# Softmax denominators of a batched attention kernel: the sum over partition quarters moved from a TensorE product to ScalarE copies and VectorE additions

## The chip, the cores and the metric

One Trainium2 core runs the whole kernel. The time is device microseconds (us) of one launch; the number that counts is the median over runs. The core has five instruction queues that run at the same time[...]: TensorE (PE, matrix products; its weight loads are shown apart as PEld), VectorE (DVE), ScalarE (ACT), GpSimd (POOL) and SyncE (SP), which issues the transfers. Each queue runs its instructions in the order in which they were written; an instruction that waits holds up all that stand behind it on its engine.

## What is computed

The input is 16 batches of 1024 nodes with 256 channels, in float32, and one 1024 x 1024 adjacency matrix. Cut to what matters:

```python
diff = c_adj[:, None, :] - c_adj[:, :, None]            # channel means of the nodes
A    = abs(abs(sigmoid(diff) - 0.5) - 0.5) * 2.0
g    = relu((fea @ (adj * A_s)) * para)                 # A_s: A made symmetric
k, v = x @ kv_w                                         # 4 heads of 64 channels
out  = softmax(q @ k.T * scale) @ v                     # q = g, by heads
x    = layernorm(x + out)
h    = relu(x @ w1_loop + adj @ (x @ w1_neigh) + b1)    # graph convolution 1
h    = relu(h @ w2_loop + adj @ (h @ w2_neigh) + b2)    # graph convolution 2
x    = layernorm(x + (x + h) * 0.5)
```

## The kernel before

The batches run one after another in a software pipeline. While batch b is in its attention, the queries, keys and values of batch b + 1 are prepared, and the graph convolutions of earlier batches are run in between: the first convolution of batch b - 1 (`c1`) and the second of batch b - 2 (`c2`) are one joint product, `Joined.run`. Batches 2 to 14, thirteen of them, have all of this and take the same path through `run()`; batches 0, 1 and 15 take others.

**Attention.** The scores of a head pair and one half of the nodes make a unit; there are four (`UNITS`). A unit's exponentials lie in eight tiles of 128 x 1024, where the partition is the key node and the columns are 512 query nodes of one head and 512 of the other. VectorE adds the eight tiles up (`collect`, L776 and L778), transposes the sum in blocks of 32 x 32 (`turned_sum`, L785) and sums over 32 columns (`part_sum`, L791). So `den_part` holds, for each unit, 32 columns on 128 partitions: the 128 partitions are four quarters of 32, each with a partial sum over a quarter of the key nodes. The denominators are the sums over the four quarters. `denominators` (L846) makes them with one TensorE product: `fold`, a 128 x 128 matrix of ones at places that agree modulo 32, times `den_part`, into a PSUM tile; then two reciprocals (L857) take the half of the columns that belongs to each head into `rden`. `add_output` (L859) multiplies the attention's output by `rden` and adds it to the activations.

**The order around the change.** In `both_units(1, ...)` the last unit's output (`av`, L803) is transposed (L835) as soon as TensorE has it, then `part_sum` of that unit follows, then the function `third`: two `scalar_tensor_tensor` instructions on VectorE, `q.times_adj(0)` and `q.times_adj(TJ)` (L613), for the next batch. GpSimd then works at `both.left` (L1323 to L1326) and `q.left` (L661 to L664), eight additions and subtractions of 128 x 512. `both.run` issues seven products of four matrix instructions each (eight records), into three PSUM tiles named `first`, `second` and `third`. What matters here is its beginning: ScalarE fills `third` with a stored sum (L1353); product 1 goes into `first`; ScalarE copies `first` to `p1` (L1355); product 2 is added onto `third`; product 6 is added onto `first`, and so it may not start before `p1` has been copied. At the point `turn_to(1)`, between product 1 and product 2, stand the likeness functions of the next batch on ScalarE (L607, L608), `att.denominators(0, 1)` and `att.add_output(0)`.

**Buffers.** All tiles of 128 x 1024 come from one pool of 31 buffers (`row_tile`). The schedule is written by hand, but which of the 31 buffers a tile gets is settled when the program is built. A tile waits for the last instructions that used its buffer's former tile. `p1` is half of such a row tile (`snap`), and the adjacency rows that `times_adj` reads are such tiles too. The pool `work` with the tag `o` has one buffer.

A float32 matrix product shows in the profile as two records.

Of the kernel before, what the change touches and what calls it, by code (L numbers as in the profile page):

```python
# [10 lines left out]
F32 = mybir.dt.float32  # L11
# [7 lines left out]
def kernel(  # L19
# [31 lines left out]
    nc = tc.nc  # L51

    B, N, C = x.shape
    P = 128
    NT = N // P
    NC = C // P
    HEADS = 4
    HD = C // HEADS
    HID = w1_loop.shape[1]
    FB = 512  # L60
    NJ = N // FB
    TJ = FB // P
# [7 lines left out]
    S = 32  # L70
    NB = N // S

    LIFT = 32.0
    UNITS = [(pair, j) for pair in range(NC) for j in range(NJ)]
    Q = P // S
# [3 lines left out]
    work = ctx.enter_context(tc.tile_pool(name="work", bufs=1))  # L79
# [88 lines left out]
    def sum_inner_weights():  # L168
        t = row_tile("w1_sums")
        a11, a12, a21, a22 = (w[:, cc, :] for w in (w1n_sb, w1l_sb) for cc in range(NC))  # L170
        s1, s2, s3, s4 = (t[:, ts(n, P)] for n in range(4))
        nc.gpsimd.tensor_add(s1, a21, a22)
        nc.gpsimd.tensor_sub(s2, s1, a11)
        nc.gpsimd.tensor_sub(s3, a11, a21)
        nc.gpsimd.tensor_sub(s4, a12, s2)
        nc.sync.dma_start(out=w1_sums, in_=t[:, 0:FB])
# [35 lines left out]
    def store(n, rows):  # L212
        for h in range(2):
            nc.sync.dma_start(out=far_adj[n][h], in_=rows[h])
# [10 lines left out]
    def adj_sums(quarters, k):  # L225
        for step in adj_sum_steps(quarters, k):
            step()

    def adj_sum_steps(quarters, k):

        w11, w12, w21, w22 = (of_rows(quarters[ij], k) for ij in QUARTERS)
        t13, t24 = (row_tile(f"adjT_{n}_{k}") for n in (13, 24))
        t = {1: t13[:, 0:FB], 3: t13[:, FB:N], 2: t24[:, 0:FB], 4: t24[:, FB:N]}

        def put(n, a, b):
            nc.vector.tensor_sub(t[n], a, b)
            nc.sync.dma_start(out=far_adj[n][k // 2][:, ts(k % 2, FB)], in_=t[n])

        return (lambda: (put(1, w12, w11), put(3, w22, w12)), lambda: put(2, w22, t[1]), lambda: put(4, w21, t[2]))
# [9 lines left out]
    def channel_major(blocked, name):  # L249

        dst = work.tile([P, NC, N], F32, tag="xT", name=name, bufs=2)
        for cc in range(NC):
            nc.vector.transpose(dst[:, cc, :], blocked[cc])
        return dst
# [90 lines left out]
    def by_node(t):  # L345
        return t.rearrange("p (bn r) -> p bn r", r=S)
# [382 lines left out]
    class Attention:  # L729
# [116 lines left out]
        def denominators(self, *pairs):  # L846
# [8 lines left out]
            for s in range(2):  # L855
                rows = slice(s * HD, (s + 1) * HD)
                nc.vector.reciprocal(rden[rows], den[rows, :, s, :])  # L857

        def add_output(self, pair):  # L859
            o = by_node(self.o.pop(NJ * pair))  # L860
            nc.vector.tensor_mul(o, o, self.rden[:, ts(pair, NB)].unsqueeze(2).to_broadcast([P, NB, S]))
            dst = by_node(self.xB[pair])
            nc.vector.tensor_add(dst, dst, o)
# [541 lines left out]
    def run():  # L1405
# [11 lines left out]
        q = Queries(0, x_first)  # L1417
# [47 lines left out]
        for b in range(B):  # L1465
            more = b + 1 < B
            att = Attention(b, xB, qT, kT, v)
            c1, c2, c3 = (convs.get(b - k) for k in (1, 2, 3))
            both = Joined(c1, c2) if c2 else None
# [4 lines left out]
            if more:  # L1474
                q = (FastQueries if c1 else Queries)(b + 1, xb)
# [6 lines left out]
            def weigh_first():  # L1482
                q.times_adj(0)
                q.times_adj(TJ)
                q.right(0)

            def two_units(pair, before_second=lambda: None):
                u = NJ * pair
                att.outputs(u, half_psum, turned=False)
                att.turn(u)  # L1490
                att.outputs(u + 1, turned=False)
                before_second()
                att.turn(u + 1)

            if more and not c1:
                att.both_scores(0)
                clip()
                NodeSums(q, xb, str(b + 1)).all()
                two_units(0)
                att.both_scores(1)  # L1500
                for t in range(3):
                    q.load(t)
                    q.weigh(t)
                two_units(1)
            elif more and not both:
                att.scores(0)
                att.outputs(0)
                NodeSums(q, xb, str(b + 1)).all()
                kv = KeysValues(b + 1, channel_major(blocked, f"xT_{b + 1}"))
                att.scores(1)  # L1510
                kv.sums()
                att.add(0)
                att.outputs(1)
                for t in (0, TJ):
                    q.load(t)
                c1.inner()
                q.left(nc.gpsimd)
                for t in (0, TJ):
                    q.likeness(t)
                for ij, n in QUARTERS.items():  # L1520
                    store(n, quarters[ij])
                c1.first(quarters, lambda: (att.add(1), adj_sums(quarters, 1), adj_sums(quarters, 2), weigh_first()))
                c1.turn_blocks()
                att.scores(2)
                att.outputs(2)
                for t in (1, TJ + 1):
                    q.load(t)
                    q.likeness(t)
                    q.times_adj(t)
                sum_inner_weights()  # L1530
                att.scores(3)
                for t in (2, TJ + 2, 3, TJ + 3):
                    q.load(t)
                for t in (2, TJ + 2, 3, TJ + 3):
                    q.likeness(t)
                q.right(1)
                att.add(2)
                att.outputs(3)
            elif more:
                nodes = None  # L1540

                def sums():
                    nonlocal nodes
                    nodes = NodeSums(q, xb, str(b + 1))
                    if c3:
                        c3.squares_aside()
                    c2.load_x()
                    c1.load_inner()

                def summed():  # L1550
                    c1.inner_sums()
                    if c3:
                        c3.deviation_aside()

                def turn_next():
                    nonlocal xT_next
                    xT_next = channel_major(blocked, f"xT_{b + 1}")

                xT_next = None

                def before_convolution():
                    both.fetch("00", "10")
                    for t in (0, TJ):
                        q.load(t)
                        q.likeness(t)
                    c1.load_t1()
                    both.fetch(2, 3)

                att.both_units(0, sums, lambda: nodes.turn(), summed=summed)
                nodes.line()  # L1570
                nodes.row()
                c1.fast_inner(turn_next)
                att.both_units(1, before_convolution, third=lambda: (q.times_adj(0), q.times_adj(TJ)))
                both.left(nc.gpsimd)
                q.left(nc.gpsimd, blocked)
                kv = KeysValues(b + 1, xT_next)
                both.fetch(1)
                for t in (1, TJ + 1):
                    q.load(t)
                both.fetch(4, "11")  # L1580

                def more_weights():
                    for t in (2, TJ + 2, 3, TJ + 3):
                        q.load(t)
                        q.likeness(t)
                    if c3:
                        c3.finish_aside(out[b - 3])

                both.run({1: (lambda: q.likeness(1), lambda: q.likeness(TJ + 1), lambda: att.denominators(0, 1),
                              lambda: att.add_output(0)),  # L1590
                          2: (lambda: att.sum_output(0), lambda: att.add_output(1)),
                          6: (lambda: q.right(0),),
                          4: (lambda: att.sum_output(1), lambda: q.times_adj(1), lambda: q.times_adj(TJ + 1)),
                          3: (more_weights, lambda: q.right(1))},
                         last=nc.gpsimd)
                c1.turn_blocks()
                if b + 2 < B:
                    c2.sums_aside()
            else:
                att.both_units(0, c1.load_inner, summed=c1.inner_sums)  # L1600
                c1.fast_inner()
                att.both_units(1, third=lambda: att.add_pairs(0))
# [57 lines left out]
            elif more:  # L1660
# [11 lines left out]
                first, second, third = adj_sum_steps(quarters, 3)  # L1672
# [17 lines left out]
        both = Joined(c1, c2)  # L1690
# [16 lines left out]
    with tc.manual_schedule():  # L1707
        run()
# [14 lines left out]
    with tc.If(count < P):  # L1723
        with tc.For_i(0, B, 1) as b:
            xb = load_x(b, "z")
            xT = channel_major(load_blocked(b, "z"), "xT_z")
            q = Queries("z", xb)
# [50 lines left out]
```

## Time and profile before

| | us |
|---|---|
| median of 3 runs (2111.35 to 2114.17) | 2112.22 |
| the profiled execution | 2112.32 |
| its span in the profile | 2110.5 |
| PE busy | 2096.5 (99%) |
| DVE busy | 1890.5 (90%) |
| ACT busy | 1247.0 (59%) |
| POOL busy | 364.4 (17%) |

The busy times are of the span. The span is 1.8 us shorter than the profiled execution. The granted TensorE clock is 0.999 of full speed. In the windows of the timeline every line is one instruction or a run of like ones: start, duration of the run from its first start to its last end, engine, source line, operation, out<-in, shapes and count; in brackets stands how long the engine was idle before it, and what ended that.

### The profile page before, as it was taken

Reading aid. Unit: us, or ns where it says so; the run is one execution under the profiler, and the core shown is the slowest. Engines: PE = TensorE matmul, PEld = TensorE weight load, DVE = VectorE, ACT = ScalarE, POOL = GpSimd, SP = SyncE. Lnnn points to the kernel's source line nnn. Section 1 sums busy time; section 2 is a strip of 40 time slices with the busy share of each in tenths; the row PEclk is TensorE's granted clock in tenths of the full one; section 3 lists DMA queues with packets and bytes.
Section 4 is the critical chain, followed back from the end, with each engine's and each line's share of the span. In section 5 each row is a group of like instructions: output and inputs, shape, how many; then the busy total and the mean of one; then the engine's idle time right before and its main releaser. Section 6 shows DMA issues by size and latency. Waiting matters only on the chain.

```text
span 2110.5 us, 24762 instructions
## 1 busy us (share of the span) xinstructions
PE 2096.5 (99%) x8360; PEld 996.7 (47%) x8360; DVE 1890.5 (90%) x2226; ACT 1247.0 (59%) x2112; POOL 364.4 (17%) x224
## 2 busy tenths in 40 slices
PE   9999999999999999999999999999999999999998
PEld 5354434445354453544535444354443534445355
DVE  6899998989989899898998989989899898989885
ACT  5844574556756566564765747557475584655523
POOL 2011103131021311213122031210312103131022
PEclk9999999999999999999999999999999999999999
DMA  9495756766648776477865768656586564966455
GB/s 220 114 184 185 146 142 199 139 215 146 173 167 160 241 132 195 155 143 241 142 204 153 142 221 174 204 132 155 195 175 216 144 155 173 183 216 131 145 186 175
DMA packets 688694, 364.99 MB, mean 173 GB/s; under 512 B 550704, under 2 KB 629936, under 8 KB 688560
## 3 DMA queue, kind: packets, MB, share of 16 engines
q1 hardware_dynamic: 688288, 363.07, 67.0%
q8 instruction: 68, 1.11, 0.2%
q14 instruction: 66, 0.54, 0.1%
q10 hardware_dynamic: 272, 0.26, 0.0%
HBM read 305.46 MB, written 57.80 MB: 172 GB/s over the span
## 4 chain that ended last, share of the span: by engine, by line
PE 97%; DVE 2%; DMA 0%; issue 0%; SPq 0%; ACT 0%; DVEq 0%; POOLq 0%
PE s L757 21%; PE av L803 20%; PE hu_ps L1332 17%; PE g_ps L702 16%; PE v_ps L463 5%; PE k_ps L459 5%; PE in_ps L997 4%; PE hu_ps L1134 4%; PE g_ps L621 3%; DVE acc L778 1%; PE h_ps L1045 1%; PE u_ps L1074 1%; PE h_ps L1134 1%; PE t_ps L971 0%; DMA x<-in_x_dram 0%
## 5 line engine op out<-in xcount | busy, mean ns | idle before, releaser
L778 DVE TENSOR_TENSOR acc<-acc,pr 128x1024 f32<-128x1024 f32 x384 | 481.4, 1254 | 34.0 <-DVE acc L776 0.9
L757 PE MATMUL s<-qT,kT 64*128 64x512 f32 x2048 | 448.7, 592 | 0.0
L803 PE MATMUL av<-pr,v 128*64 128x512 f32 x2048 | 447.0, 594 | 0.0
L764 ACT ACTIVATE pr<-s 128x1024 f32<-128x1024 f32 x392 | 390.9, 1117 | 58.1 <-PE s L757 58.1
L757 PEld LDWEIGHTS s<-qT,kT 64*128 64x128 f32 x2048 | 195.2, 187 | 241.0 <-issue 191.2
L803 PEld LDWEIGHTS av<-pr,v 128*64 128x64 f32 x2048 | 144.0, 137 | 297.3 <-issue 269.2
L1332 PE MATMUL hu_ps<-adj,R 128*128 128x512 f32 x480 | 213.6, 592 | 0.0
L376 POOL TENSOR_TENSOR rstd<-rstd,neg_half 128x32 f32<-128x32 f32 x16 | 88.3, 5522 | 564.5 <-DVE rstd L374 564.5
L613 DVE SCALAR_TENSOR_TENSOR wg<-wg,adj 128x1024 f32<-128x1024 f32 x128 | 169.0, 1359 | 3.6 <-ACT wg L608 3.6
L762 ACT ACTIVATE pr<-s 128x512 f32<-128x512 f32 x240 | 142.5, 703 | 0.0
L607 ACT ACTIVATE wg<-c_row,c_sums 128x1024 f32<-128x1024 f32 x120 | 139.7, 1164 | 2.6 <-DVE accB L785 1.0
L1332 PEld LDWEIGHTS hu_ps<-adj,R 128*128 128x128 f32 x480 | 90.0, 190 | 107.1 <-issue 99.2
L608 ACT ACTIVATE wg<-wg 128x1024 f32<-128x1024 f32 x128 | 135.5, 1058 | 4.1
L1332 PE MATMUL hu_ps<-adj,t 128*128 128x512 f32 x240 | 109.2, 598 | 0.0
L702 PE MATMUL g_ps<-wg,x 128*128 128x512 f32 x224 | 107.7, 593 | 0.0
L702 PE MATMUL g_ps<-T,xB 128*128 128x512 f32 x208 | 107.3, 597 | 0.0
L702 PE MATMUL g_ps<-wg,xB 128*128 128x512 f32 x208 | 106.2, 592 | 0.0
L1355 ACT COPY snap<-hu_ps 128x512 f32<-128x512 f32 x15 | 8.8, 586 | 157.4 <-PE hu_ps L1332 136.1
L1195 POOL TENSOR_TENSOR rstd<-rstd,neg_half 128x8 f32<-128x8 f32 x12 | 19.6, 1637 | 457.2 <-DVE rstd L1194 457.2
L1323 POOL TENSOR_TENSOR R<-h 128x512 f32<-128x512 f32 x14 | 20.7, 1480 | 433.5 <-PE av L803 407.3
L776 DVE TENSOR_TENSOR acc<-pr,pr 128x1024 f32<-128x1024 f32 x64 | 78.0, 1219 | 14.1 <-ACT pr L764 12.9
L785 DVE STREAM_TRANSPOSE accB<-acc 128x1024 f32<-128x1024 f32 x64 | 79.7, 1245 | 3.1
(301 smaller groups left out, 3298.9 us busy)
## 6 DMA issues: line engine op xcount, KB each, us to landing
adj<-adjT SPq DMA_DIRECT2D x210, 512.0 KB
adj<-in_adj_dram SPq DMA_DIRECT2D x128, 512.0 KB
para<-in_L_gnn_para_dram SPq DMA_DIRECT2D x32, 512.0 KB
xB_a<-in_x_dram SPq DMA_DIRECT2D x128, 128.0 KB
x1d<-xB_a SPq DMA_DIRECT2D x128, 128.0 KB
x<-x1d SPq DMA_DIRECT2D x16, 1024.0 KB
xB<-in_x_dram SPq DMA_DIRECT2D x120, 128.0 KB
x<-in_x_dram SPq DMA_DIRECT2D x15, 1024.0 KB
```

The costliest lines, as they stand in the source:

```text
L459: nc.tensor.matmul(dst, self.a[0][n], self.w[n], start=not again, stop=True, skip_group_check=again)
L463: nc.tensor.matmul(dst[:, ts(t, P)], self.w[n][:, ts(t, P)], self.a[1][n], start=not again and t == 0, stop=True, skip_group_check=again o ...
L607: nc.scalar.activation(wg, self.c_row, AF.Abs, bias=self.c_col[:, t:t + 1], scale=-1.0)
L608: nc.scalar.activation(wg, wg, AF.Tanh, scale=-0.5 / C)
L613: nc.vector.scalar_tensor_tensor(wg, wg, 1.0, self.adj.pop(t), op0=ALU.add, op1=ALU.mult)
L702: nc.tensor.matmul(self.p[n], x_n[:, k, :], w_n, start=(k == 0), stop=(k == TJ - 1))
L757: nc.tensor.matmul(halves[s], self.kT[rows, pair, ts(mt, P)], self.qT[rows, pair, ts(j, FB)], start=True, stop=True)
L762: nc.scalar.activation(pr[:, ts(s, FB)], halves[s], AF.Exp)
L764: nc.scalar.activation(pr, ps, AF.Exp)
L778: nc.vector.tensor_add(self.acc, self.acc, prs[mt])
L803: nc.tensor.matmul(pav[s * HD:(s + 1) * HD, :], self.v[:, mt, pair * P + s * HD:pair * P + (s + 1) * HD], prs[mt][:, ts(s, FB)], start=(mt ...
L1332: nc.tensor.matmul(dst, self.x[n][:, k, :], of_rows(rows, k), start=(start and k == 0), stop=(k == TJ - 1), skip_group_check=again)
```

## The change

Three functions take the place of `denominators(0, 1)` in batches 2 to 14. The other batches keep the product.

- `den_shift`, first thing in `third`: two ScalarE copies of 64 x 64 bring the columns of each head from the other 64 partitions.
- `den_halves`, between the two `times_adj`: two VectorE additions of 64 x 64 add them to the partitions' own columns. After it, partition halves are summed, and each head's columns lie on the head's own 64 partitions.
- `den_quarters`, first thing at `turn_to(1)`: four ScalarE copies of 32 x 64 exchange neighbouring quarters, one VectorE addition of 128 x 64 sums them, one reciprocal of 128 x 64 fills `rden`.

```diff
+        def den_shift(self):
+            t = work.tile([P, FB], F32, tag="o", name=f"den_{self.b}")
+            self.den = [t[:, ts(k, NC * NB)] for k in range(3)]
+            part = self.part.rearrange("p u (s h) -> p u s h", s=2)
+            for s in range(2):
+                mine, other = slice(s * HD, (s + 1) * HD), slice((1 - s) * HD, (2 - s) * HD)
+                dst = self.den[0][mine].rearrange("p (u h) -> p u h", u=len(UNITS))
+                nc.scalar.copy(dst, part[other, :, s, :])
+
+        def den_halves(self):
+            part = self.part.rearrange("p u (s h) -> p u s h", s=2)
+            for s in range(2):
+                mine = slice(s * HD, (s + 1) * HD)
+                first, both = (self.den[k][mine].rearrange("p (u h) -> p u h", u=len(UNITS)) for k in range(2))
+                nc.vector.tensor_add(both, first, part[mine, :, s, :])
+
+        def den_quarters(self):
+            for a in range(Q):
+                nc.scalar.copy(self.den[2][a * S:(a + 1) * S], self.den[1][(a ^ 1) * S:((a ^ 1) + 1) * S])
+            nc.vector.tensor_add(self.den[1], self.den[1], self.den[2])
+            nc.vector.reciprocal(self.rden, self.den[1])
...
-                att.both_units(1, before_convolution, third=lambda: (q.times_adj(0), q.times_adj(TJ)))
+                att.both_units(1, before_convolution, third=lambda: (att.den_shift(), q.times_adj(0), att.den_halves(), q.times_adj(TJ)))
...
-                both.run({1: (lambda: q.likeness(1), lambda: q.likeness(TJ + 1), lambda: att.denominators(0, 1),
+                both.run({1: (att.den_quarters, lambda: q.likeness(1), lambda: q.likeness(TJ + 1),
                               lambda: att.add_output(0)),
```

## The prediction

> **What bounds the kernel now.** I read the page first, its busy times and the chain that ended last:
>
> ```profile
> PE 2096.5 (99%) x8360; PEld 996.7 (47%) x8360; DVE 1890.5 (90%) x2226; ACT 1247.0 (59%) x2112; POOL 364.4 (17%) x224
> ...
> PE 97%; DVE 2%; DMA 0%; issue 0%; SPq 0%; ACT 0%; DVEq 0%; POOLq 0%
> ```
>
> TensorE sets the end, almost without a gap. So an instruction taken from TensorE is worth its full time in the row of products, and whatever makes TensorE wait is paid in full. Next the table of waits: TensorE's matrix instructions wait 5.0 us in all (1.9 + 1.5 + 0.7 + 0.4 + 0.3 + 0.2), 0.4 of it, once, in a joint product. Then the timeline of one of the thirteen batches where the change sits; the others look alike (a period of 129.47 us). TensorE:
>
> ```profile
> 1101.95 3.70 PE L1332 MATMUL hu_ps<-adj,t 128*128 128x512 f32 x8
> 1105.49 0.38 PE L851 MATMUL den_ps<-den_part,fold 128*128 128x128 f32 x2
> 1105.71 3.60 PE L1332 MATMUL hu_ps<-adj,t 128*128 128x512 f32 x8
> 1109.14 10.46 PE L1332 MATMUL hu_ps<-adj,R 128*128 128x512 f32 x24
> ```
>
> Products 1, 2 and 6 follow each other with the denominators' product between the first two. Eight records take 1109.14 - 1105.71 = 3.43 us, so product 1 fills up to 1101.95 + 3.43 = 1105.38, and L851 costs 1105.71 - 1105.38 = 0.33 us. ScalarE and VectorE in the same stretch:
>
> ```profile
> 1094.48 0.58 ACT L1353 COPY hu_ps<-in 128x512 f32<-128x512 f32 x1
> 1105.69 0.59 ACT L1355 COPY snap<-hu_ps 128x512 f32<-128x512 f32 x1 [10.62 <-PE hu_ps L1332]
> 1106.17 1.16 ACT L607 ACTIVATE wg<-c_row,c_sums 128x1024 f32<-128x1024 f32 x1
> ...
> 1112.78 0.59 ACT L1363 COPY snap<-hu_ps 128x512 f32<-128x512 f32 x1 [2.23 <-PE hu_ps L1332]
> ```
>
> ```profile
> 1102.07 0.72 DVE L835 STREAM_TRANSPOSE o<-av 128x512 f32<-128x512 f32 x1 [1.29 <-PE av L803]
> 1102.71 1.18 DVE L791 TENSOR_REDUCE den_part<-accB 128x32 f32<-128x1024 f32 x1
> 1103.80 3.73 DVE L613 SCALAR_TENSOR_TENSOR wg<-wg,adj 128x1024 f32<-128x1024 f32 x2
> 1107.46 1.11 DVE L857 RECIPROCAL rden<-den_ps 64x64 f32<-64x64 f32 x2
> 1108.61 1.22 DVE L861 TENSOR_TENSOR o<-o,rden 128x1024 f32<-128x1024 f32 x1
> 1109.87 2.18 DVE L863 TENSOR_TENSOR xB_a<-xB_a,o 128x1024 f32<-128x1024 f32 x1
> 1112.08 0.69 DVE L1358 TENSOR_TENSOR snap<-snap,hu_ps 128x512 f32<-128x512 f32 x1
> ...
> 1123.13 0.69 DVE L1376 TENSOR_TENSOR uT<-snap,hu_ps 128x512 f32<-128x512 f32 x1 [4.13 <-PE hu_ps L1332]
> ```
>
> The copy of `p1` (L1355) starts as soon as product 1 ends, and is done 2.9 us before product 6 starts. VectorE idles 4.13 us before L1376, which is the cover for anything that it does later than before. GpSimd:
>
> ```profile
> 1102.97 1.27 POOL L661 TENSOR_TENSOR xB<-x 128x512 f32<-128x512 f32 x1
> 1104.32 2.13 POOL L662 TENSOR_TENSOR xB<-xB,x 128x512 f32<-128x512 f32 x1
> 1106.42 2.25 POOL L663 TENSOR_TENSOR xB<-x 128x512 f32<-128x512 f32 x1
> 1108.63 2.33 POOL L664 TENSOR_TENSOR xB<-x,xB 128x512 f32<-128x512 f32 x1
> ```
>
> Alone such a subtraction takes 1.27 us; these take up to 2.33. Of the two L613 the first took 1.52 us and the second, started at 1105.25, took 2.29, where an undisturbed one takes 1.22. Put the ends in a row: L661 1104.24, first L613 1105.33, L662 1106.45, second L613 1107.54, L663 1108.67, L861 1109.83, L664 1110.96, L863 1112.05. Each comes 1.08 to 1.16 us after the one before: the two engines take turns.
>
> [...]
>
> **The change part by part.**
>
> *Removed:* L851, -0.33 us on TensorE in 13 batches, -4.3 us. Two reciprocals from PSUM, 1.11 us of VectorE.
>
> *`den_shift`:* two ScalarE copies[...]. They wait for L791's end at 1103.89. Behind them now stands the fill of `third` (L1353, before at 1094.48):[...] Product 2's first weight load would be at about 1105.06.[...]
>
> *`den_halves`:* two additions of N = 64[...]. They stand between the two L613, in the middle of the taking of turns.
>
> *`den_quarters`:* [...] one reciprocal for two, 0.56 for 1.11.[...]
>
> *Moved without a line in the diff:* the buffers. In the semaphore waits of the two built programs, `p1`'s row tile takes a different one of the 31. Before, its buffer came from the transposed sum, last read by L791 (1103.89), long over. Now it comes from the adjacency rows of node tile TJ, last read by the second L613. This holds in all 13 batches. So the chain is now second L613, then copy of `p1`, then product 6; and in front of that L613 stand the two small additions. The transfers that took other buffers now wait for L785, L791 and the first L613 (1105.33), or for the unit's `av`, where they waited for product 1 (1105.6): not later, no cost.
>
> When does the second L613 end? [...]
> L662 ends 1106.45 as before; first addition 1106.54[...]; L663 1.13 later, 1107.67; second addition 1107.76; L664 1108.89; L613 1.08 later, 1109.97. The copy of `p1` starts 0.05 later (ScalarE's start after a VectorE end, as at L1036: 0.04) and takes 0.59: 1110.61. TensorE resumes 0.13 after a release (L1005 to L997: 1071.30 to 1071.43): product 6 starts at 1110.74 instead of 1109.14, +1.60 us, with the 0.33 already taken off. In two of the 13 batches GpSimd runs 0.37 us later (the first L613 took 1.88 there), +1.97. Sum: 11 x 1.60 + 2 x 1.97 = 21.5 us.
>
> Will GpSimd get in? L663 starts at 1106.42. The second addition can start only some 0.08 us before the first one's end (second L613 against the first), at 1106.46. The same 40 ns repeat for L664 against L613. That is narrow but on GpSimd's side both times.
>
> What is late next: the four copies stand behind `p1`, so VectorE's addition waits until about 1111.2, and L1358 comes at about 1114.8 instead of 1112.08. The likeness work ends near 1115.6, so the copy of product 6 (L1363) is done at 1116.2; product 5, which needs it, starts about 1117.6. VectorE would reach L1376 by 1121.2, and product 4 ends about 1124.7. All of it is covered; without that cover, each us would be one of TensorE's.
>
> Sum: 2112.3 (profiled execution) + 21.5 = 2133.8; on the median, 0.1 lower, 2133.7 us.
>
> **The rivals.** *The wait costs nothing (other side).* If the additions take no turn of their own, because they are small or run on 64 partitions, the second L613 ends between 1107.54 and 1107.8, `p1` is ready by 1108.45, and product 6 keeps its time, 1108.81. Then only the 0.33 us remain: 2112.2 - 4.3 = 2107.9. It decides below 1108.0 as the end of L613. For it: no row of before shows so small an addition against GpSimd. Against it: L861 and L863, other two-input forms, take turns. [...] Then one GpSimd instruction gets in: additions done 1106.64, L663 1107.77, L613 1108.85, product 6 at 1109.62, +0.48 a batch: 2118.4. The 40 ns speak against it; batches can also differ, which gives times between 2118 and 2134. *ScalarE is the bound:* if the small copies are much dearer than priced, `third` is late for product 2; but product 6 is later still for `p1`'s sake, so copies of up to 1.3 us apart ((1110.74 - 3.43 - 0.13 - 0.58 - 1103.93)/2) add nothing to the first case; in the no-stall case they would cost from 0.37 us apart on.
>
> **How the numbers follow.** The full taking of turns 0.55, own range 2129 to 2138; one turn or a mixture 0.24; no stall 0.17; worse than the first case 0.04. The predicted time is the first case's. The range 2116 to 2138 takes in the first two, 0.79, and the near part of the last. About 0.2% (4.2 us) is what a measurement can tell from no change; the no-stall case lies at that edge, so it gives 0.10 to faster and 0.07 to same. Slower: 0.83.
>
> **What would show it.** Right: L851 gone in 13 batches; a gap of about 1.9 us on TensorE before product 6, released by the copy of `p1`; in front of that copy ScalarE idle, released by L613; the second L613 ending near 1110.0, with the three GpSimd instructions L662 to L664 all ended before it; product 2 right behind product 1. Wrong: the second L613 ending near 1107.6, or additions that don't wait. A gap before product 2 would speak for ScalarE, one after product 4 for VectorE.

## The result, and the profile after

| | before | after |
|---|---|---|
| median, us | 2112.16 (2111.35 to 2114.17) | 2135.98 (2135.34 to 2137.13) |
| span of the profiled execution, us | 2110.5 | 2134.1 |
| granted TensorE clock | 0.999 | 0.998 |

Five runs of each give a ratio of 1.0113, with a 95% interval of 1.0102 to 1.0125: the change makes the kernel slower by 23.8 us. The forecast was 2133.7 us.

In the changed kernel the lines behind the new functions stand 22 further down: the joint products are L1354, the fill of `third` L1375, the copy of `p1` L1377. New are L866 (`den_shift`), L873 (`den_halves`), and L877, L878 and L879 (the copies, the addition and the reciprocal of `den_quarters`).

The page of the changed kernel, its busy times and the shares of the chain that ended last:

```profile
PE 2098.5 (98%) x8334; PEld 994.9 (47%) x8334; DVE 1904.7 (89%) x2252; ACT 1264.7 (59%) x2190; POOL 336.9 (16%) x224
...
PE 94%; DVE 2%; issue 2%; POOL 1%; DMA 1%; ACT 0%; SPq 0%; POOLq 0%; DVEq 0%
```

TensorE has lost its 26 records (13 products), yet the span is 23.6 us longer. Most of the difference is time in which TensorE waits: 26.4 us in the table of waits, where it was 5.0. Its largest row (line, what released it: us in total, times, longest):

```profile
PE hu_ps L1354 <- issue: 22.1, 13, 2.0
```

Thirteen waits, one in each changed batch, at a joint product. One of these batches in the timeline; TensorE first:

```profile
1113.14 7.13 PE L1354 MATMUL hu_ps<-adj,t 128*128 128x512 f32 x16
1121.91 10.54 PE L1354 MATMUL hu_ps<-adj,R 128*128 128x512 f32 x24 [1.64 <-issue]
```

Products 1 and 2 now run as one row of 16 records, and then 1.64 us pass before product 6. ScalarE in the same stretch:

```profile
1115.10 0.51 ACT L866 COPY den<-den_part 64x64 f32<-64x64 f32 x2 [9.35 <-DVE den_part L791]
1115.52 0.58 ACT L1375 COPY hu_ps<-in 128x512 f32<-128x512 f32 x1
1121.23 0.58 ACT L1377 COPY snap<-hu_ps 128x512 f32<-128x512 f32 x1 [5.13 <-PE hu_ps L1354]
1121.84 1.00 ACT L877 COPY den<-den 32x64 f32<-32x64 f32 x4
```

The copy of `p1` (L1377) is what ends TensorE's wait: it is done at 1121.81, and product 6 starts at 1121.91. ScalarE stood idle for 5.13 us ahead of it. The bracket names product 1, but product 1 had ended near 1116.8; what came last is on VectorE:

```profile
1113.26 0.72 DVE L835 STREAM_TRANSPOSE o<-av 128x512 f32<-128x512 f32 x1 [1.30 <-PE av L803]
...
1114.99 1.51 DVE L613 SCALAR_TENSOR_TENSOR wg<-wg,adj 128x1024 f32<-128x1024 f32 x1
1116.42 2.50 DVE L873 TENSOR_TENSOR den<-den,den_part 64x64 f32<-64x64 f32 x2
1118.96 2.19 DVE L613 SCALAR_TENSOR_TENSOR wg<-wg,adj 128x1024 f32<-128x1024 f32 x1
1122.87 0.22 DVE L878 TENSOR_TENSOR den<-den 128x64 f32<-128x64 f32 x1 [1.72 <-ACT den L877]
```

The second L613 ends at 1121.15, and the copy starts 0.08 us later. The two small additions took 2.50 us together; L878, on twice as many partitions, took 0.22 us where GpSimd is idle. GpSimd beside them:

```profile
1115.50 2.12 POOL L662 TENSOR_TENSOR xB<-xB,x 128x512 f32<-128x512 f32 x1
1117.59 1.26 POOL L663 TENSOR_TENSOR xB<-x 128x512 f32<-128x512 f32 x1
1118.81 1.26 POOL L664 TENSOR_TENSOR xB<-x,xB 128x512 f32<-128x512 f32 x1
```

The ends in a row: first L613 1116.50, L662 1117.62, first addition 1117.70, L663 1118.84, second addition 1118.92, L664 1120.07, second L613 1121.15. Each addition ends 0.08 us after a whole GpSimd instruction.

The times below are counted from the start of L835 in the batch, so that batches and kernels can be laid side by side:

| after L835's start, us | before | forecast | after, 11 batches | after, 2 batches |
|---|---|---|---|---|
| second L613 ends | 5.47 | 7.90 | 7.89 to 7.97 | 8.24, 8.26 |
| product 2 starts | 3.64 | | 3.42 | 3.42 |
| product 6 starts | 7.08 | 8.67 | 8.66 (8.74 in batch 2) | 9.00, 9.02 |
| period from batch to batch | 129.47 | +1.60 | 131.12 (+1.65) | 131.46 (+2.0) |

Eleven times 1.65 and twice 2.0 are 22.2 of the span's 23.6 us. Another 1.2 lie ahead of the first changed batch: its L835 starts at 326.48 us instead of 325.26. There TensorE's clock stood at half for 3.41 us. The windows view (columns: stretch, length, busy time of PE, PEld, DVE, ACT and POOL with counts, TensorE clock, DMA share, GB/s):

```profile
295.27:298.68 3.41, 3.41 (x6) 0.91 (x7) 1.77 (x2) 0.58 (x1) 0.00 (x0) 0.50 0.00 0
```

In the kernel before, the clock is 1.00 in this stretch. Seven of the eleven traces of this study have such a stretch near 295 us, and their first L835 starts at 326.4 to 327.3 us; in the other four (before, e1, e7 and e9) it starts at 324.6 to 325.4. The kernel without any sum (e5) has it, a changed kernel with one addition more (e9) has not: it is not put down to the change. The last section comes back to it.

### The profile page after: what moved, and what is told of

It reads as the page before. It is cut to its first block, busy times and chain, and to the rows that moved or that the text cites. A ratio compares the mean times of both kernels' runs of the same rounds, so it can differ in the third digit from the quotient of the medians.

```text
span 2134.1 us, 24787 instructions
## 1 busy us (share of the span) xinstructions
PE 2098.5 (98%) x8334; PEld 994.9 (47%) x8334; DVE 1904.7 (89%) x2252; ACT 1264.7 (59%) x2190; POOL 336.9 (16%) x224
## 4 chain that ended last, share of the span: by engine, by line
PE 94%; DVE 2%; issue 2%; POOL 1%; DMA 1%; ACT 0%; SPq 0%; POOLq 0%; DVEq 0%
PE s L757 20%; PE av L803 19%; PE g_ps L702 16%; PE hu_ps L1354 16%; PE v_ps L463 5%; PE k_ps L459 5%; PE in_ps L1019 4%; PE hu_ps L1156 4%; PE g_ps L621 3%; DVE acc L778 1%; PE h_ps L1067 1%; PE u_ps L1096 1%; PE h_ps L1156 1%; PE t_ps L993 0%; ACT pr L764 0%
## 5 line engine op out<-in xcount | busy, mean ns | idle before, releaser
L1354 PE MATMUL hu_ps<-adj,R 128*128 128x512 f32 x480 | 214.6, 594 | 22.1 <-issue 22.1
L613 DVE SCALAR_TENSOR_TENSOR wg<-wg,adj 128x1024 f32<-128x1024 f32 x128 | 168.6, 1348 | 4.0 <-ACT wg L608 3.6
L1354 PEld LDWEIGHTS hu_ps<-adj,R 128*128 128x128 f32 x480 | 88.9, 190 | 133.4 <-issue 130.1
L1354 PE MATMUL hu_ps<-adj,t 128*128 128x512 f32 x240 | 107.1, 598 | 0.0
L866 ACT COPY den<-den_part 64x64 f32<-64x64 f32 x26 | 6.3, 243 | 121.8 <-DVE den_part L791 121.5
```

The costliest lines, as they stand in the source:

```text
L613: nc.vector.scalar_tensor_tensor(wg, wg, 1.0, self.adj.pop(t), op0=ALU.add, op1=ALU.mult)
L1354: nc.tensor.matmul(dst, self.x[n][:, k, :], of_rows(rows, k), start=(start and k == 0), stop=(k == TJ - 1), skip_group_check=again)
```

## The experiments

The theory: GpSimd takes a turn before each small addition; this makes the second L613 late; and that matters only because the copy of `p1` waits for that L613, for the sake of its buffer. The rivals: the six ScalarE copies cost the time; or the additions do so as VectorE work; or the sum over quarters is dear wherever it stands. Each median stands beside that of the kernel before in the same round of runs; the ratio, with its 95% interval, is over all these runs and not of the two medians.

### The additions behind the second `times_adj` (e1)

```diff
-third=lambda: (att.den_shift(), q.times_adj(0), att.den_halves(), q.times_adj(TJ))
+third=lambda: (att.den_shift(), q.times_adj(0), q.times_adj(TJ), att.den_halves())
```

> The two additions of den_halves stand behind both times_adj instead of between them; the copy of p1 still waits for the second of these. [...] the second times_adj ends 5.5 us after the start of the unit's transposition (before: 5.47, changed kernel: 7.90), the copy is done at 6.1, product 6 starts at 6.86 without a gap; what is left is the removed product, 0.22 us in 13 batches: 2109.3 us, 26.7 below the changed kernel. Rival, that the six small ScalarE copies and the later reciprocal hold TensorE: unchanged copies, so 2130 us or more.

Measured: 2110.01 us beside 2112.95, 0.9987 of before (0.998 to 0.9993). Timeline of VectorE in one batch:

```profile
1101.06 0.72 DVE L835 STREAM_TRANSPOSE o<-av 128x512 f32<-128x512 f32 x1 [1.30 <-PE av L803]
...
1102.80 3.72 DVE L613 SCALAR_TENSOR_TENSOR wg<-wg,adj 128x1024 f32<-128x1024 f32 x2
1106.44 2.51 DVE L873 TENSOR_TENSOR den<-den,den_part 64x64 f32<-64x64 f32 x2
```

The additions still take 2.51 us, but the second L613 ends 5.46 us after L835's start, product 6 starts at 6.85 with no gap, and the period is 129.27 us. The copy of `p1` still starts 0.08 us after the second L613, so its wait is in place. All copies and additions are there, and the kernel is slightly faster than before. The copies fall as a cause, and so does the amount of VectorE work: what costs is the place of the additions.

### Another buffer for `p1` (e2)

The additions stay where the change put them; `p1` goes into the stored sum's tile, whose half ScalarE has just read for the fill of `third`.

```diff
             p1, u1, u3, p7 = s12[:, 0:FB], s12[:, FB:N], s34[:, 0:FB], s34[:, FB:N]
+            if c1.loops is not None:
+                p1 = c1.loops[:, 0:FB]
```

> The changed kernel, but p1 is written into the first half of the loops tile, which the fill of third has just read, so that it waits for no times_adj; the additions stay between the two times_adj. Taking turns plus the buffer's wait: the second times_adj still ends 7.9 us after the transposition's start, but nobody on TensorE's path waits for it: no gap before product 6, 2109.3 us. Rival, that VectorE's own delay of 2.4 us reaches TensorE by some other way: a gap later in the joint product, 2120 to 2136 us.

Measured: 2109.85 us beside 2112.95, 0.9987 (0.998 to 0.9994). Timelines of VectorE and of TensorE in one batch, its L835 at 1102.23:

```profile
1107.95 2.19 DVE L613 SCALAR_TENSOR_TENSOR wg<-wg,adj 128x1024 f32<-128x1024 f32 x1
```

```profile
1109.08 10.46 PE L1354 MATMUL hu_ps<-adj,R 128*128 128x512 f32 x24
```

The second L613 is as late as in the changed kernel (7.91 after L835's start), but product 6 starts at 6.85, without a wait. The buffer is the link.

### One operand of the additions in PSUM (e3)

```diff
             self.den = [t[:, ts(k, NC * NB)] for k in range(3)]
+            self.den[0] = bank_psum(f"den_ps_{self.b}")[:, 0:NC * NB]
```

> The changed kernel, but den_shift copies into PSUM, so that each addition of den_halves has one SBUF input only; order and the wait of p1 stay. [...] the additions run at once while GpSimd works (0.2 us each instead of 1.28 and 1.20), the second times_adj ends at 5.5 us as in the kernel before, no gap before product 6: 2109.3 us. Rival, that any two more VectorE instructions at this place let GpSimd in twice: times_adj ends at 7.9 us again and 2136 us.

Measured: 2110.56 us beside 2112.95, 0.9988 (0.998 to 0.9996). Timeline of VectorE (here the additions are L874; L835 starts at 1102.66):

```profile
1105.83 0.45 DVE L874 TENSOR_TENSOR den<-den_ps,den_part 64x64 f32<-64x64 f32 x2
1106.31 1.80 DVE L613 SCALAR_TENSOR_TENSOR wg<-wg,adj 128x1024 f32<-128x1024 f32 x1
```

Same instructions, same place, same sizes, but only one input in SBUF: both together take 0.45 us instead of 2.50, the second L613 ends at 5.45, and the gap is gone. The copy of `p1` still starts 0.08 us after it. So it is the second SBUF input that makes an addition wait for GpSimd here: with it one addition took 1.28 us and the other 1.20, without it the two together 0.45.

### No sum at all (e5), and the additions alone (e7)

In e5, `den_part` of before goes straight into the reciprocals. This leaves out three quarters of the terms of every denominator.

```diff
+        def no_sum(self):
+            part = self.part.rearrange("p u (s h) -> p u s h", s=2)
+            rden = self.rden.rearrange("p (u h) -> p u h", u=len(UNITS))
+            for s in range(2):
+                rows = slice(s * HD, (s + 1) * HD)
+                nc.vector.reciprocal(rden[rows], part[rows, :, s, :])
...
-                both.run({1: (lambda: q.likeness(1), lambda: q.likeness(TJ + 1), lambda: att.denominators(0, 1),
+                both.run({1: (lambda: q.likeness(1), lambda: q.likeness(TJ + 1), att.no_sum,
```

> The kernel before without any sum over the quarters: the two reciprocals read den_part itself, so the denominators lack three quarters of their terms and the output is not the reference's. Neither product nor copies nor additions. If the product was worth what products 2 and 6 moved by in the last three runs, 0.22 us in 13 batches, this takes 2.9 us off: ratio 0.9986, the same as with the copies in place. If the 0.33 us of the prediction were right: 4.3 us, 0.9980. If the small copies and additions still cost something in those runs, this is faster than they are.

Measured: 2110.07 us beside 2111.93, 0.9986 (0.9979 to 0.9993). Product 6 starts at 6.85 and the period is 129.22 us. So the TensorE product was worth 0.22 us a batch by the start of product 6 and 0.25 by the period, about 3 us in all, and in this schedule that is all that moving the sum elsewhere can win. Since e1, e2 and e3 reach the same time (their periods are 129.27, 129.26 and 129.23 us), their copies and additions cost nothing that can be measured.

In e7, two additions whose result nobody reads are put into the kernel before, which keeps its product:

```diff
-third=lambda: (q.times_adj(0), q.times_adj(TJ))
+third=lambda: (q.times_adj(0), att.idle_adds(), q.times_adj(TJ))
```

> The kernel before, with its product and its buffers, and two additions of 64 x 64 between the two times_adj whose result nobody uses. Taking turns plus the buffer's wait: the second times_adj ends at 7.9 us here too, but p1 waits for an older reader of its buffer, so product 6 keeps its time: 2112 us, no change. Rival, that the late times_adj alone is enough: 2134 to 2136 us.

Measured: 2112.4 us beside 2111.93, 0.9998 (0.999 to 1.0007). The second L613 ends at 7.91, as late as in the changed kernel, and product 6 starts at 7.08, as before: the copy of `p1` does not wait for that L613 here, it starts at 3.62, as product 1 ends. A late L613 alone costs nothing. The loss needs both, the turns and the buffer.

### GpSimd's subtractions out of the way (e6)

`q.left`, four GpSimd instructions, is moved behind `both.run(...)`, so that the additions meet an idle GpSimd.

```diff
                 both.left(nc.gpsimd)
-                q.left(nc.gpsimd, blocked)
...
                          last=nc.gpsimd)
+                q.left(nc.gpsimd, blocked)
```

> The changed kernel, but GpSimd's q.left (L661 to L664) is issued behind the joint product instead of before it; the additions, their place and the wait of p1 stay. Taking turns: no GpSimd instruction is there, the second times_adj ends some 4.5 us after the transposition's start, no gap before product 6: about 2109 us if the four subtractions find room later, up to 2115 if they disturb VectorE there. Rival, that the additions themselves or the copies make times_adj late: it ends at 7.9 us and 2136 us.

Measured: 2134.57 us beside 2111.93, 1.01 (1.0084 to 1.0115). Half of the expectation came in: in the timeline of VectorE the second L613 ends at 4.59, and product 6 starts at 6.85 without a gap. But the period is 131.23 us. The same four instructions now collide with VectorE's work further on. Timelines of VectorE and of TensorE:

```profile
1116.97 0.46 DVE L873 TENSOR_TENSOR den<-den,den_part 64x64 f32<-64x64 f32 x2
...
1136.55 1.64 DVE L1146 TENSOR_TENSOR last<-h1T,last 128x512 f32<-128x512 f32 x1
1138.12 1.75 DVE L1147 TENSOR_TENSOR last<-uT 128x512 f32<-128x512 f32 x1
...
1144.74 0.68 DVE L1178 TENSOR_TENSOR h<-h,hu_ps 128x512 f32<-128x512 f32 x1
```

```profile
1145.47 1.16 PE L1156 MATMUL hu_ps<-w2l_sb,last 128*128 128x128 f32 x8 [1.67 <-DVE h L1178]
```

In the changed kernel L1146 and L1147 take 0.69 and 0.68 us; here VectorE comes out of them 2.1 us late, counted from L1398. TensorE does not wait for `last`, which is complete at 1139.87. It waits for L1178, further back in VectorE's row and late by the same 2.1 us: L1178 reads the PSUM tile that the second convolution's next product is added onto, ends at 1145.42, and that product starts 0.05 us later, after a wait of 1.67 us. The two additions alone took 0.46 us, which is the undisturbed price. The expectation had allowed for some disturbance there, up to 2115 us; its error was not to look up what the moved instructions meet.

### More additions (e4, e9, e8)

Each addition of `den_halves` twice (e4); the second one twice, three in all (e9); each four times (e8). The edit of e8; in e9 the range is `1 + s`, and in e4 the line of the addition stands there twice:

```diff
-                nc.vector.tensor_add(both, first, part[mine, :, s, :])
+                for _ in range(4):
+                    nc.vector.tensor_add(both, first, part[mine, :, s, :])
```

> Each of the two additions of den_halves is done twice (the same result). Taking turns: after the two turns of L663 and L664 GpSimd has nothing left to do here, so two more additions cost only their own time and their waits on each other, about 0.45 us a batch: second times_adj ends at 8.35 us, 2136 + 6 = 2142 us. Rival, that every small addition at this place costs some 1.2 us by itself: 2136 + 13 x 2.4 = 2167 us.

> Each addition four times (the same result). With twice, product 6 came 0.53 us later than in the changed kernel, and in 11 of 13 batches the products behind the gap ran at half pace for a while, which cost another 1.7 us. If that is a loss of TensorE's clock after a gap of more than some 2.2 us: four more additions at 0.26 us lengthen the gap by 1.05 us, the clock falls in all 13 batches, and the loss by the clock stays 1.7 us: 2160 + 13.6 + 3.4 = 2177 us. If the loss grows with the gap: 2190 us or more.

> The second addition is done twice, so that the second times_adj ends 0.26 us later than in the changed kernel and TensorE's gap is 0.26 us longer, between that of the changed kernel (no loss of clock in 13 batches) and that of the two doubled additions (loss in 11). If the clock holds up to there: 2136 + 13 x 0.26 = 2139.4 us. If it falls as with twice: about 2157 us. In between, with some of the batches slowed, 2142 to 2152 us.

The columns of L613 and of product 6 count from L835's start and give most batches:

| | median, us | second L613 ends | product 6 starts | TensorE clock |
|---|---|---|---|---|
| changed kernel | 2135.98 | 7.90 | 8.66 | 0.998 |
| e9, three | 2158.4 | 8.16 | 8.92 | 0.989 |
| e4, four | 2160.11 | 8.42 | 9.19 | 0.990 |
| e8, eight | 2175.7 | 9.43 | 10.19 | 0.989 |

By the start of product 6 the theory holds: behind L664, the last GpSimd instruction, an addition has nobody to give way to, and four additions cost 0.53 us more than two, not two turns more. The rival, a turn for every addition, falls. But the times were far above the expectation of e4 (2142): 24.1 us more than the changed kernel, of which 13 x 0.53 explains 6.9. The rest lies behind the gap. Product 6 and its followers in the timeline of TensorE, first e9, then a batch of the changed kernel whose gap is even longer:

```profile
1130.99 12.23 PE L1355 MATMUL hu_ps<-adj,R 128*128 128x512 f32 x24 [1.91 <-issue]
```

```profile
1515.60 10.54 PE L1354 MATMUL hu_ps<-adj,R 128*128 128x512 f32 x24 [1.99 <-issue]
```

24 records take 12.23 us instead of 10.54: 1.69 us are lost after the gap. The windows view of e9, columns as above:

```profile
1128.69:1132.11 3.42, 1.51 (x4) 0.67 (x4) 1.67 (x3) 1.72 (x6) 0.20 (x1) 1.00 1.01 408
1132.11:1135.52 3.41, 3.41 (x5) 1.36 (x5) 3.31 (x5) 3.35 (x4) 0.00 (x0) 0.50 0.11 39
1135.52:1138.93 3.41, 3.41 (x9) 1.49 (x8) 3.38 (x4) 2.00 (x3) 0.00 (x0) 1.00 0.00 0
```

The granted clock is 0.50 for 3.41 us, and 1.00 before and after; in the changed kernel it is 1.00 all through the like stretch. In e9 this happens in 12 of 13 batches, in e4 in 11. In e9: 13 x 0.26 + 12 x 1.70 = 23.8 us above the changed kernel; measured 22.4, with runs from 2153.78 to 2160.45. In e4: 6.9 + 11 x 1.70 = 25.6; measured 24.1. In e8, with gaps of about 3.2 to 3.5 us, five batches lose nothing, four about 1.6 and four about 3 us. The expectation had 1.7 in each of the 13; that the sum came out near it (2177) is luck.

## Why the prediction was right

It said slower, by the full taking of turns, and that is what the traces and runs show.

**Which wait ends last.** That `p1` had moved to a buffer last read by the second L613 was the step on which all rested, and it had no line in the diff. e2 shows it by taking that link away and nothing else; e7, where the additions are in place and the link is not, shows it from the other side.

**The turns.** L613, L662, addition, L663, addition, L664, L613: the order came as predicted in all 13 batches, the end at 7.89 to 7.97 in 11 of them (7.90 said) and about 0.35 later in the two where GpSimd runs late (0.37 said). GpSimd's lead of some 40 ns held each time: L663 starts 4.33 us after L835's start, and VectorE could have started 0.08 us before the first addition's end at 4.44. e3 shows the cause. Each addition ended 0.08 us after the GpSimd instruction ahead of it (0.076 to 0.086 in the 13 batches); the 0.09 that the forecast took was shown by no trace of before. The rival of one turn fell, the one without a stall too.

**Product 6.** Forecast at +1.60 and +1.97 us, measured at +1.58 and +1.93. This makes 11 x 1.58 + 2 x 1.93 = 21.2 us, where 21.5 was said. Two small errors cancel: the copy starts 0.08 us after L613 instead of 0.05, and TensorE 0.10 after the copy instead of 0.13. Missing from the sum was the restart: behind the gap the 24 records take 10.54 instead of 10.46 us, 13 times some 0.075 us, which makes 22.2.

**L851 was mis-sized.** The forecast took 0.33 us from the start of product 2. The product was worth 0.22: product 1 itself takes 3.54 us instead of 3.43, at the change from the product before it, which had been booked on L851. So product 2 starts 0.11 us later than the forecast had it, and the gap behind it reads 1.64 us where 1.9 was said; another 0.16 us are the modelled end of the last record, which reaches past the point where a next one would start. In the first case this has no effect on the time, since product 6 waits for `p1` anyhow. The rival without a stall would have come out at 2109.3, not at 2107.9; e1, e2 and e3 lie at 2109.85 to 2110.56.

**ScalarE.** The small copies took 0.24 us each and stand 0.25 to 0.27 us apart, so they do not overlap each other; the two of `den_shift` take 0.51 us together, and the fill of `third` starts 0.42 us after the first. What the forecast took for these copies no trace of before showed. `third` was ready 2.84 us after L835's start, in time for product 2, which starts at 3.42.

**What was said to be covered was covered.** The copies of `den_quarters` had their input at 1118.92, but stand behind the copy of `p1` on ScalarE and so started at 1121.84. The addition L878 waits 1.72 us for them (some 1.2 in the forecast), and no wait of TensorE follows from that.

**The clock was left out, and here luck came in.** The forecast was 2.3 us short. The batches account for 0.7 of it; 1.2 are the stretch at half clock ahead of them, which is not put down to the change. The prediction had no term for what a gap does to TensorE's clock. Gaps of 1.64 us cost no clock, but three additions instead of two, with a gap 0.26 us longer, cost 22 us more: that lies outside the range, and nothing in the prediction told the two cases apart.

Open is which part of the change moved `p1`'s buffer. With additions alone (e7) and with the product removed alone (e5) the copy of `p1` starts as product 1 ends, 3.62 us after L835's start, so neither edit alone makes the choice of the changed kernel.

## What to carry to other kernels

When a change allocates or frees anything, compare the waits of the two built programs, not only the diff: the 22 us came from a tile that took another buffer of its pool. A small VectorE instruction with two SBUF inputs cost a whole GpSimd instruction here, where GpSimd had work queued (1.20 to 1.28 us in place of some 0.22); put it where its successors are not awaited (e1), or give it one input in PSUM (e3). Where GpSimd's work is moved out of the way, ask first what it will meet there. And do not price a gap of TensorE by its length alone: here, from 1.86 us on, it could cost another 1.7.

## What was not expected of the hardware

**The clock after a gap.** After some gaps TensorE's clock falls to half for a stretch of 3.41 us (in four batches of e8 for two in a row), and one stretch costs about 1.7 us. The length of the gap alone does not decide it: gaps of 1.91 us cost 1.69 us in e9, one of 1.99 us nothing in the changed kernel. Where the gap lies in time does. In each trace the lowered stretches start whole multiples of 3.4133 us apart, to within 0.004 us: their starts lie on a grid. In the changed kernel the clock falls at 295.27 and, behind TensorE's last products, at 2128.23 us, 537 such steps apart. All gaps of TensorE above 0.9 us in the eleven traces, laid on it (the first 30 us and the last 60 before TensorE's end left out; a gap begins at the modelled end of a record):

| length of the gap, us | begins so far behind a mark of the grid, us | gaps | followed by a lowered stretch |
|---|---|---|---|
| 1.63 to 1.72 | anywhere | 24 | 0 |
| 1.86 to 3.53 | 0.13 to 1.39 | 37 | 37 |
| 1.86 to 3.53 | 1.42 to 3.30 | 13 | 0 |
| 1.86 | 0.07 | 1 | 0 |
| 2.16 | 3.38 | 1 | 1 |

Of the 38 gaps that cost, 37 begin 0.13 to 1.39 us behind a mark of the grid, and the clock falls at the next mark. A gap of one length shows it best: all eleven kernels have a wait of 1.86 us near 292 us. Seven times it began 0.25 to 1.12 us behind a mark, and half clock followed near 295 us; four times it began at 0.07 or at 1.92 to 3.30, and none followed. In e9 the batches are 133.10 us apart and 39 steps of the grid are 133.12, so each gap lies nearly where the one before it lay, and the loss repeats. The changed kernel's gaps are either too short or, the two of 2.0 us, begin at 2.95 and 3.20.

What decides within a step stays open: 1.86 us without a product were enough where they began 0.25 to 1.12 us behind a mark, while a gap that began at 1.42 left the remaining 1.99 us of its step idle and cost nothing.

**Turns between back-to-back instructions.** GpSimd got its turn between two VectorE instructions that follow each other at once, in all 13 batches: L663 and L664 start 0.11 to 0.13 us before the end of the addition ahead of them, and the next VectorE instruction could have started 0.08 us before that end (second L613 against the first, before: 1105.25 and 1105.33). That is a lead of some 40 ns by the starts in the trace.
